# Moving the next pair's transposes and differences inside a Strassen-form pair of products (two graph layers, one Trainium2 core)

## Chip, cores and metric

The kernel runs on one core of one Trainium2 chip. The metric is the device time of one execution in microseconds. Six runs of the kernel before gave a median of 1068.01 us (1065.46 to 1069.62).

## The reference, cut to what matters

There are 2708 nodes with 1024 features in f32 and a sparse 0/1 adjacency matrix.

```
q, k, v = x@W_q.T + b_q, x@W_k.T + b_k, x@W_v.T + b_v
z    = where((q@k.T / 32) * adj == 0, -10000, (q@k.T / 32) * adj)
x    = layernorm(x + relu(softmax(z, axis=1) @ v))          # layer 0
x    = layernorm(x + adj @ (x @ weight) + bias)             # layer 1
```

## The kernel before, in words

**Staging.** The rows of `adj` become lists of column numbers, and the rows are sorted by how many they have, into 22 blocks of 128 rows (`SLOTS` is the list length that each block allows: 15 for block 0, down to 0 for block 21). Attention is computed only on listed neighbours: their rows of x are fetched by indirect gathers on GpSimd (POOL, `gather_slot`, L349), scored on VectorE (DVE, L813) and summed with their weights (L870). Layer 1 gathers rows of the layer-0 result `x1_d` and sums them (`sum_rows`, L1226, DVE L1238 and L1241). The weighted row sum r of a block is then multiplied by a 1024 x 1024 weight matrix on TensorE (PE).

**From one row sum to a product.** `flip` (L709) turns r: eight PE transposes of 128 x 128 into two PSUM tiles `tr` (L716), each copied by ScalarE (ACT) to the tile rT (L717). `tr` has three buffers in all (`p_tr`), rT two for each place in a pair.

**Pairs.** Most blocks are multiplied two at a time. `turn_pair` (L977) turns both row sums and then forms four matrices on DVE, `s_all` (L988 to L991, S[0] to S[3]) from the quarters a11, a12 (first block's rT) and a21, a22 (second block's). `s_all` has one buffer. `pair_products` (L1013) makes seven half products of four f32 matmuls each, into four PSUM banks, in the order a11·w11, a12·w21, S[1]·t2, S[0]·t1, S[2]·t3, S[3]·w22, a22·t4; w are quarters of the weights and t differences of them. Behind several of them DVE reads a bank: `add` (L1009, L1011) or `whole` (L1011 in layer 0, L1278 in layer 1). S[1]·t2 accumulates in the bank of a11·w11, so it may start only when `add(to[0][0], pa, base[0][0])` (L1022) has read that bank. In layer 1 the `base` is xr, the block's own row of x1 added on top of the bias: ACT copies the bias to xr (L1251), and POOL adds the gathered row (L1252).

**Order.** In layer 0 the list `steps` (L1089) ends with seven pairs, here pair 0 to pair 6: (7,20), (19,18), (17,8), (16,11), (15,10), (9,14), (13,12). In each step the loop (L1119) finishes the pair before (`finish_pair`), runs gather jobs, turns the blocks of this step and of the next (L1149), and only then emits this pair's products. In layer 1 the list `units` (L1221) has unit 0 (block 20 alone) and ten pairs, unit 1 to unit 10. Step i (L1309) finishes unit i-1, turns unit i+1, fetches xr of unit i+1, emits the row sums of unit i+3, and then the products of unit i.

The program is written with a framework that orders each engine's instructions itself: every instruction has a priority by its place in the program, an earlier one first, and `tc.high_priority(URGENT)` lifts some, such as `add`. An instruction is put into its engine's queue when its inputs and its buffers are free by the framework's own estimate of time; on the chip each queue then runs in that order. So the place in the program is a preference, and the trace shows what came of it. SyncE (SP) only starts the weight and bias loads here.

Of the kernel before, what the change touches and what calls it, by code (L numbers as in the profile page):

```python
# [80 lines left out]
def sparse_part(ctx, tc, x, xT, adj, wqT, wkT, wvT, bq, bk, bv, w1, b1, out):  # L81
# [29 lines left out]
    with es:  # L111
# [863 lines left out]
        halves_turned = []  # L975

        def turn_pair(flips, pool):  # L977

            A = []
            for k, flip_to in enumerate(flips):  # L980
                rT = (pool if k else wp).tile([P, DC, P], F32, name="rT", bufs=2)
                A.append(flip_to(rT))
            if len(flips) == 1:
                return A, None
            (a11, a12), (a21, a22) = [(a[:, :DC // 2], a[:, DC // 2:]) for a in A]
            s_all = wm_pool.tile([P, 4, DC // 2, P], F32, name="s_all", tag="m3")
            S = [s_all[:, i] for i in range(4)]
            nc.vector.tensor_add(S[0], a21, a22)  # L988
            nc.vector.tensor_sub(S[1], S[0], a11)
            nc.vector.tensor_sub(S[2], a11, a21)  # L990
            halves_turned.append(nc.vector.tensor_sub(S[3], a12, S[1]))  # L991
            return A, S

        def differences():
            return [wm_pool.tile([P, DC // 2, HALF], F32, name=f"t{k}", tag=f"m{k - 2}") for k in (2, 3, 4)]
# [14 lines left out]
            with tc.high_priority(URGENT):  # L1010
                nc.vector.tensor_add(to, acc, what)  # L1011

        def pair_products(A, S, w, ts, base, to, whole, first_alone=False):  # L1013

            (w11, t1), (w21, w22) = w
            t2, t3, t4 = ts
            (a11, a12), a22 = halves_of_turned(A[0]), halves_of_turned(A[1])[1]
            pa, pb, pc = bank(), bank(), bank()  # L1020
            half_products(pa, a11, w11, stop=False)
            add(to[0][0], pa, base[0][0])  # L1022
            half_products(pb, a12, w21)
            whole(0, 0, pb, to[0][0])
            if first_alone:
                half_products(pc, S[0], t1, stop=False)
                add(to[1][1], pc, base[1][1])
                half_products(pa, S[1], t2, start=False, stop=False)
                add(to[0][1], pa, base[0][1])
                half_products(pc, S[3], w22, start=False)  # L1030
                whole(0, 1, pc, to[0][1])
                half_products(pa, S[2], t3, start=False)
                whole(1, 1, pa, to[1][1])
                pd = bank()
                add(to[1][0], pa, base[1][0])
                products.append(half_products(pd, a22, t4))
                whole(1, 0, pd, to[1][0])
# [12 lines left out]
        def halves_of_turned(a):  # L1050
            return a[:, :DC // 2], a[:, DC // 2:]

        def project_pair(pair, A, S):
            ts = [(xb_pools[0] if k else wp).tile([P, D], F32, name="t", bufs=2 + k) for k in range(2)]
            bias = halves_of(bias_bc)

            def whole(k, h, acc, what):
                add(halves_of(ts[k])[h], acc, what)

            pair_products(A, S, wv_q, wv_t, [bias, bias], [halves_of(t) for t in ts], whole, pair == pairs[-1])  # L1060
            return ts

        def finish_pair(pair, ts):
# [44 lines left out]
        def turn0(b):  # L1108
# [3 lines left out]
                return rT  # L1112
            return flip_shares([got["hub"], got[0]]) if b == 0 else flip(got[b])

        credit = -STEP
        turned, done0 = {}, set(last)
        pending = None
        left_y = NB - FAMILY
        for i, (kind, b) in enumerate(steps):  # L1119
            if pending is not None:  # L1120
                pending[0](*pending[1:])
                credit -= END * (2 if pending[0] is finish_pair else 1)
                pending = None
            credit += STEP if kind != "p" else 2 * STEP - P_END
            step[0] = i
            for entry in joining[:]:
                if i >= entry[1] + 2:
# [12 lines left out]
            for c in [c for st in steps[i:i + 3] for c in blocks_of(st) if not (left_y and c in late)]:  # L1140
                while c not in done0 and c not in got and c != 0:
                    credit -= run_job()
            while 0 in jobs and i >= 15:
                credit -= run_job()
            while jobs and credit > 0 and len([c for c in got if c not in done0 and c not in ALONE and c != "hub"]) < (RB - 1 if left_y else RB):
                if left_y and len(jobs) <= late_jobs:
                    break
                credit -= run_job()
            for k, c in steps[i:i + 2]:  # L1149
                if k != "y" and c not in turned and not (left_y and k == "p"):  # L1150
                    turned[c] = turn0(c) if k == "v" else turn_pair([lambda rT, r=got[b_]: flip(r, rT) for b_ in c], xb_pools[0])
                    done0.update(blocks_of((k, c)))
            if kind == "y":
                if b == NB - 5:
                    row_constants(1)
                y_block(b)
                credit -= Y_END
                left_y -= 1
                if left_y == 0:
                    xa.release()  # L1160
                    xb_pool = tc.alloc_tile_pool(name="xb", bufs=1, side="right", reuse_waits="tile")
                    xb_pools.append(xb_pool)
                    xb_bc.append(xb_pool.tile([P, D], F32, name="xb_bc"))
                    bcast_rows(xb_bc[0], xbT)
            elif kind == "v":
                xr = gather_x(x, b)
                pending = finish0, b, (project_mean if b in last else project)(turned[b], wv_q), xr
            else:
                for b_ in b:
                    pair_x[b_] = gather_x(x, b_)  # L1170
                pending = finish_pair, b, project_pair(b, *turned[b])
        w1_q = quarters_of("w1")
        for i in range(2):
            for j in range(2):
# [96 lines left out]
        def work1(unit, A, S, xrs):  # L1271
# [14 lines left out]
            if S is None:  # L1286
                (a11, a12), x0 = halves_of_turned(A[0]), xs_[0]
                pa, pb = bank(), bank()
                half_products(pa, a11, w11, stop=False)
                add(x0[1], pa, x0[1])  # L1290
                half_products(pb, a11, t1, stop=False)
                half_products(pb, a12, w22, start=False)
                whole(0, 1, pb, x0[1])
                half_products(pa, a12, w21, start=False)
                whole(0, 0, pa, x0[0])
            else:
                pair_products(A, S, w1_q, w1_t, xs_, xs_, whole, unit == units[-1])
# [5 lines left out]
        turned1[0] = turn1(units[0], got1.pop(0))  # L1303
        follow(nc.vector.tensor_sub(t1, t1, w11), firsts[0], same=True)
        nc.vector.tensor_sub(t2, w22, t1)
        nc.vector.tensor_sub(t3, t2, w11)
# [2 lines left out]
        for i, unit in enumerate(units):  # L1309
            for p in pending:  # L1310
                finish1(*p)
            if i + 1 < len(units):
                turned1[i + 1] = turn1(units[i + 1], got1.pop(i + 1))
                xrs[i + 1] = [gather_x1(b, k) for k, b in enumerate(units[i + 1])]
            if i == 0:
                got1[2] = [sum_rows(b, k, halves_turned[-1]) for k, b in enumerate(units[2])]
            if i + 3 < len(units):
                got1[i + 3] = [sum_rows(b, k) for k, b in enumerate(units[i + 3])]
            if i == 4:
                sum_rows("hub")  # L1320
            pending = list(zip(unit, *work1(unit, *turned1.pop(i), xrs.pop(i))))
            if i == 2:
                for b in last:
                    pending.append((b, gather_x1(b), None))
# [319 lines left out]
```

## Time and profile before

The profiled execution took 1067.15 us, of which the span that the profile shows is 1065.4 us; 1.75 us lie around it.

| stretch of the span | what it is | PE busy | DVE busy | POOL busy |
|---|---|---|---|---|
| 558.00 to 746.00 (188.00 us) | layer 0, seven pairs | 184.36 us | 162.50 us | 95.86 us |
| 746.00 to 757.85 (11.85 us) | between the layers | 0.17 us | 4.46 us | 4.57 us |
| 757.85 to 860.00 (102.15 us) | layer 1, units 0 to 3 | 96.67 us | 80.68 us | 79.27 us |
| 860.00 to 960.60 (100.60 us) | layer 1, units 4 to 7 | 96.97 us | 80.71 us | 81.40 us |
| 960.60 to 1047.90 (87.30 us) | layer 1, rest of unit 7 to unit 10 | 87.25 us | 43.43 us | 32.91 us |

Busy time is the time in which an engine worked on an instruction. The timeline lists instructions in order with the time at which they began, how long they (or a run of equal ones) took, and in brackets how long the engine stood idle before and which instruction released it. An f32 matmul appears as two records, so a half product of four matmuls is a row with x8, and a turned block is a row with x8 of L716. POOL shows an idle time of 0.30 us or 0.31 us between two indirect gathers even when nothing holds it.

### The profile page before, as it was taken

The numbers are of one execution on the slowest core, as the hardware profiler recorded it, in microseconds if no ns is written. First come the engines' busy times: TensorE is split into PE (matmuls) and PEld (weight loads), VectorE is DVE, ScalarE is ACT, GpSimd is POOL, SyncE is SP. The second block draws the span as 40 slices with busy tenths as digits, with TensorE's granted clock in tenths as the row PEclk, the third lists the DMA queues.
The fourth block names the chain that finished last, engine by engine and source line by source line (L and its number), as shares of the span: only waits on it lengthen the run. The fifth ranks groups of instructions, "written<-read, shape, count | busy, mean of one in ns | idle before, by whom it ended". The sixth has DMA issues, their size and how long they took to land.

```text
span 1065.4 us, 10216 instructions
## 1 busy us (share of the span) xinstructions
PE 1005.1 (94%) x2849; PEld 473.7 (44%) x2849; DVE 849.6 (80%) x1831; ACT 425.6 (40%) x894; POOL 496.6 (47%) x397
## 2 busy tenths in 40 slices
PE   7999999999999999999999999999589999999993
PEld 6444444444443444444544444444334444454441
DVE  8799999994288889999399999965677877896532
ACT  4688788422042332214424343332323353333321
POOL 1000140057655445526157666511677787887300
PEclk9999999999999999999999999999799999999997
DMA  9555458565887656796433777726689589979701
GB/s 361 191 205 202 167 208 287 160 220 164 293 258 245 223 184 206 219 355 191 152 126 100 244 240 264 252 80 224 167 280 264 183 285 305 291 214 309 204 40 42
DMA packets 90962, 229.20 MB, mean 215 GB/s; under 512 B 18410, under 2 KB 40394, under 8 KB 88188
## 3 DMA queue, kind: packets, MB, share of 16 engines
q0 software_dynamic: 48768, 148.05, 43.6%
q1 hardware_dynamic: 42128, 80.41, 21.7%
q8 instruction: 24, 0.39, 0.1%
q14 instruction: 42, 0.34, 0.1%
HBM read 219.61 MB, written 33.68 MB: 238 GB/s over the span
## 4 chain that ended last, share of the span: by engine, by line
PE 18%; DVE 15%; issue 8%; DMA 5%; POOL 3%; ACT 1%; POOLq 0%; DVEq 0%
PE po L999 16%; DMA g<-x_d,tabs 3%; DVE r L870 3%; DVE junkv L813 2%; DVE r L1241 2%; DVE t L1011 1%; DMA yg<-y_d,tabs 1%; POOL g L349 1%; PE tr L716 1%; POOL xr L343 1%; DVE part L1241 1%; DMA g<-in_x_dram,tabs 1%; PE po L739 1%; PE tr L729 1%; POOL r L349 1%
## 5 line engine op out<-in xcount | busy, mean ns | idle before, releaser
L319 PE MATMUL po<-m_sb,xt 128*128 128x512 f32 x672 | 292.1, 593 | 3.2 <-DVE yo L323 3.2
L319 PEld LDWEIGHTS po<-m_sb,xt 128*128 128x128 f32 x672 | 126.5, 190 | 159.3 <-issue 151.1
L813 DVE SCALAR_TENSOR_TENSOR junkv<-yg,g 128x1024 uint8<-128x1024 f32 x109 | 132.9, 1219 | 32.4 <-DMA g<-in_x_dram,tabs 14.8
L349 POOL DMA_INDIRECT g<-in_x_dram,tabs x86 | 111.8, 1300 | 70.2 <-ACT r L868 20.0
L999 PE MATMUL po<-t,s_all 128*128 128x512 f32 x272 | 123.2, 595 | 4.0 <-DVE xr L1011 4.0
L1241 DVE SCALAR_TENSOR_TENSOR r<-g,valid,r 128x1024 f32<-128x1024 f32 x77 | 98.5, 1280 | 24.9 <-DMA g<-x_d,tabs 24.4
L609 PE MATMUL po<-wk_o,wq_o 128*128 128x512 f32 x256 | 110.5, 592 | 0.0
L739 PE MATMUL po<-wv,rT 128*128 128x512 f32 x224 | 97.7, 593 | 3.1 <-DVE pr L855 2.5
L775 ACT ACTIVATE junks<-t,lnm 128x1024 uint8<-128x1024 f32 (+1 forms) x41 | 47.0, 1146 | 127.2 <-DVE lnm L773 97.6
L349 POOL DMA_INDIRECT g<-x_d,tabs x67 | 78.6, 1174 | 22.7 <-issue 14.0
L563 POOL DMA_INDIRECT tab_d<-rec,pos_i x22 | 27.1, 1231 | 129.8 <-DVE pos_i L552 123.4
L870 DVE SCALAR_TENSOR_TENSOR r<-g,pr,r 128x1024 f32<-128x1024 f32 x64 | 81.8, 1279 | 5.8 <-ACT r L882 4.6
L999 PE MATMUL po<-w,rT 128*128 128x512 f32 x192 | 86.4, 599 | 0.0
L332 ACT ACTIVATE junka<-xt 128x128 f32<-128x128 f32 x176 | 53.8, 306 | 75.3 <-PE po L319 56.8
L788 ACT ACTIVATE t<-t,nmr,rstd 128x1024 f32<-128x1024 f32 (+1 forms) x41 | 50.0, 1237 | 81.2 <-DVE nmr L787 81.1
L999 PEld LDWEIGHTS po<-t,s_all 128*128 128x128 f32 x272 | 50.9, 190 | 70.5 <-issue 58.1
L224 DVE MAX8 few<-a 128x8 f32<-128x75 f32 (+3 forms) x132 | 79.2, 617 | 0.0
L609 PEld LDWEIGHTS po<-wk_o,wq_o 128*128 128x128 f32 x256 | 48.3, 190 | 59.3 <-issue 59.1
L999 PE MATMUL po<-w,s_all 128*128 128x512 f32 x160 | 72.1, 592 | 0.0
L221 DVE SCALAR_TENSOR_TENSOR a<-a,iota 128x2708 f32<-128x2708 f32 (+1 forms) x22 | 65.2, 2963 | 5.4 <-ACT junk L220 5.4
L739 PEld LDWEIGHTS po<-wv,rT 128*128 128x128 f32 x224 | 42.2, 190 | 56.0 <-issue 54.9
L717 ACT COPY rT<-tr 128x512 f32<-128x512 f32 x80 | 43.1, 586 | 52.8 <-PE tr L716 52.6
(350 smaller groups left out, 1524.4 us busy)
## 6 DMA issues: line engine op xcount, KB each, us to landing
a<-in_adj_dram SPq DMA_DIRECT2D x21, 1354.0 KB, 5.8
xt<-in_xT_dram SPq DMA_DIRECT2D x21, 512.0 KB, 5.2
y_d<-yo SPq DMA_DIRECT2D x21, 512.0 KB, 5.8
g<-in_x_dram SPq DMA_DIRECT2D x21, 512.0 KB, 7.9
wq_i<-in_wqT_dram SPq DMA_DIRECT2D x8, 512.0 KB, 8.8
wk_i<-in_wkT_dram SPq DMA_DIRECT2D x8, 512.0 KB, 10.4
wv<-in_wvT_dram SPq DMA_DIRECT2D x16, 256.0 KB, 5.6
w<-in_w_dram SPq DMA_DIRECT2D x4, 1024.0 KB, 7.6
```

What stands on the lines that cost most here:

```text
L221: nc.vector.scalar_tensor_tensor(a[:n], a[:n], 1.0, iota[:n], op0=ALU.is_equal, op1=ALU.mult)
L224: nc.vector.max(few[:n, i * 8:(i + 1) * 8], a[:n, cuts[i]:cuts[i + 1]])
L319: put = nc.tensor.matmul(po, xt[:, c, :], m_sb[c // 2][:, c % 2, k0:k1], start=(c == 0), stop=(c == DC - 1))
L332: put = nc.scalar.activation(junka, xts[b][:, c, :], AF.Copy, accum_out=xs[:, c, b:b + 1])
L349: nc.gpsimd.indirect_dma_start(out=dst[:n], out_offset=None, in_=src, in_offset=bass.IndirectOffsetOnAxis(ap=at, axis=0), bounds_check=N - ...
L609: nc.tensor.matmul(po, wq_o[i // 2][:, o, i % 2 * P:(i % 2 + 1) * P], wk_o[:, o, hs], start=(o == 0), stop=(o == DC - 1))
L739: put = nc.tensor.matmul(acc, rT[:, c, :], w[c // 4][h][:, c % 4, :], start=(c == 0), stop=(c == DC - 1))
L788: applied.append(nc.scalar.activation(t[:n], t[:n], AF.Identity, bias=nmr[:n], scale=rstd[:n]))
L813: nc.vector.scalar_tensor_tensor(junkv[:n], yg[:n, :D], scale, xg[:n], op0=ALU.mult, op1=ALU.mult, accum_out=s)
L870: nc.vector.scalar_tensor_tensor(r[:n], xg[j][:n], pr[:n, j:j + 1], r[:n], op0=ALU.mult, op1=ALU.add)
L999: put = nc.tensor.matmul(acc, a[:, k], w[:, k], start=start and k == 0, stop=stop and k == DC // 2 - 1, skip_group_check=True)
L1241: put = nc.vector.scalar_tensor_tensor(r[:n], xg[:n], ok[:n, j:j + 1], r[:n], op0=ALU.mult, op1=ALU.add)
```

## The change

The transposes of the next pair move from ahead of this pair's products to a place inside them, behind a12·w21 (`between()`). The four differences of the next pair move behind all of this pair's products (`pair_sums`). In layer 1 this puts the differences of unit i+1 behind the row sums of unit i+3 in the program; in step 0 the row sums of units 2 and 3 now both come behind the products of unit 0 and are tied to follow the last difference of unit 1 on DVE. The single unit 0 gets `between()` behind its first half product. No instruction is added or dropped.

```diff
-        def pair_products(A, S, w, ts, base, to, whole, first_alone=False):
+        def pair_products(A, S, w, ts, base, to, whole, between, first_alone=False):
...
             half_products(pb, a12, w21)
             whole(0, 0, pb, to[0][0])
+            between()
...
             for k, c in steps[i:i + 2]:
-                if k != "y" and c not in turned and not (left_y and k == "p"):
-                    turned[c] = turn0(c) if k == "v" else turn_pair([lambda rT, r=got[b_]: flip(r, rT) for b_ in c], xb_pools[0])
-                    done0.update(blocks_of((k, c)))
+                if k == "v" and c not in turned:
+                    turned[c] = turn0(c)
+                    done0.add(c)
+            if kind == "v" and steps[i + 1][0] == "p":
+                turned[pairs[0]] = turned_pair(pairs[0])
+                sums0[pairs[0]] = pair_sums(turned[pairs[0]])
...
-                pending = finish_pair, b, project_pair(b, *turned[b])
+                following = steps[i + 1][1] if i + 1 < len(steps) else None
+                pending = finish_pair, b, project_pair(b, turned[b], sums0[b], lambda: turned.update(
+                    {following: turned_pair(following)} if following else {}))
+                if following:
+                    sums0[following] = pair_sums(turned[following])
...
                 add(x0[1], pa, x0[1])
+                between()
                 half_products(pb, a11, t1, stop=False)
...
             if i + 1 < len(units):
-                turned1[i + 1] = turn1(units[i + 1], got1.pop(i + 1))
                 xrs[i + 1] = [gather_x1(b, k) for k, b in enumerate(units[i + 1])]
-            if i == 0:
-                got1[2] = [sum_rows(b, k, halves_turned[-1]) for k, b in enumerate(units[2])]
-            if i + 3 < len(units):
+            if 0 < i < len(units) - 3:
                 got1[i + 3] = [sum_rows(b, k) for k, b in enumerate(units[i + 3])]
             if i == 4:
                 sum_rows("hub")
-            pending = list(zip(unit, *work1(unit, *turned1.pop(i), xrs.pop(i))))
+            pending = list(zip(unit, *work1(unit, turned1.pop(i), sums1.pop(i), xrs.pop(i), lambda: turned1.update(
+                {i + 1: turn1(units[i + 1], got1.pop(i + 1))} if i + 1 < len(units) else {}))))
+            if i + 1 < len(units):
+                sums1[i + 1] = pair_sums(turned1[i + 1])
+            if i == 0:
+                for u in (2, 3):
+                    got1[u] = [sum_rows(b, k, halves_turned[-1]) for k, b in enumerate(units[u])]
```

`pair_sums` holds the old second half of `turn_pair`, L985 to L992, unchanged; `turned_pair` marks the pair's blocks as done and calls `turn_pair`.

More of the change, by code (lines that the diff above doesn't have):

```diff
@@ L982, in turn_pair, with pair_sums @@
                 A.append(flip_to(rT))
-            if len(flips) == 1:
-                return A, None
+            return A
+        def pair_sums(A):
+            if len(A) == 1:
+                return None
             (a11, a12), (a21, a22) = [(a[:, :DC // 2], a[:, DC // 2:]) for a in A]
@@ L991, in turn_pair @@
             halves_turned.append(nc.vector.tensor_sub(S[3], a12, S[1]))
-            return A, S
+            return S
         def differences():
@@ L1051, in halves_of_turned, with project_pair @@
             return a[:, :DC // 2], a[:, DC // 2:]
-        def project_pair(pair, A, S):
+        def project_pair(pair, A, S, between):
             ts = [(xb_pools[0] if k else wp).tile([P, D], F32, name="t", bufs=2 + k) for k in range(2)]
@@ L1058, in whole @@
                 add(halves_of(ts[k])[h], acc, what)
-            pair_products(A, S, wv_q, wv_t, [bias, bias], [halves_of(t) for t in ts], whole, pair == pairs[-1])
+            pair_products(A, S, wv_q, wv_t, [bias, bias], [halves_of(t) for t in ts], whole, between, pair == pairs[-1])
             return ts
@@ L1113, in turn0, with turned_pair @@
             return flip_shares([got["hub"], got[0]]) if b == 0 else flip(got[b])
+        def turned_pair(pair):
+            done0.update(pair)
+            return turn_pair([lambda rT, r=got[b_]: flip(r, rT) for b_ in pair], xb_pools[0])
+        sums0 = {}
         credit = -STEP
@@ L1269, in turn1, with work1 @@
                               for b, r in zip(unit, rs)], cp)
-        def work1(unit, A, S, xrs):
+        def work1(unit, A, S, xrs, between):
             ts = [wp.tile([P, D], F32, name="t", tag="t" if k % 2 == 0 else "yg") for k, _ in enumerate(unit)]
@@ L1296, in work1 @@
             else:
-                pair_products(A, S, w1_q, w1_t, xs_, xs_, whole, unit == units[-1])
+                pair_products(A, S, w1_q, w1_t, xs_, xs_, whole, between, unit == units[-1])
             return ts, sums
@@ L1303, in sparse_part @@
         turned1[0] = turn1(units[0], got1.pop(0))
+        sums1 = {0: pair_sums(turned1[0])}
         follow(nc.vector.tensor_sub(t1, t1, w11), firsts[0], same=True)
```

## The prediction

> **What bounds the kernel now.** I read the engine totals first, then the 40 slices, then PE's waits in the two pair stretches, then the timelines of PE, DVE, ACT and POOL there.
>
> ```profile
> PE 1005.1 (94%) x2849; PEld 473.7 (44%) x2849; DVE 849.6 (80%) x1831; ACT 425.6 (40%) x894; POOL 496.6 (47%) x397
> ...
> PE   7999999999999999999999999999589999999993
> ...
> POOL 1000140057655445526157666511677787887300
> ```
>
> PE is busy nearly everywhere, and since the change adds and drops no instruction, it can only win PE's idle gaps or open new ones. PE's waits from 558 to 1048 us (total, times, longest) say what gaps there are:
>
> ```profile
> PE tr L716 <- DVE r L1238: 12.2, 2, 11.7
> PE po L999 <- DVE xr L1011: 4.0, 4, 2.0
> PE tr L716 <- DVE r L870: 2.9, 4, 1.3
> PE tr L716 <- ACT rT L717: 2.0, 1, 2.0
> PE tr L716 <- DVE r L1241: 2.0, 1, 2.0
> PE tr L729 <- DVE r L1241: 0.6, 1, 0.6
> ```
>
> The 11.7 is the seam between the layers, where the last scatter and first gathers run; the change doesn't touch it. What remains, 12.2 + 4.0 + 2.9 + 2.0 + 2.0 + 0.6 - 11.7 = 12.0 us, is about the most that can be won (stretched records hide a little more, as in unit 0 below).
>
> PE's timeline of layer 0 (pairs 4 and 5) shows where:
>
> ```profile
> 666.34 3.60 PE L999 MATMUL po<-wv,rT 128*128 128x512 f32 x8
> 671.16 1.06 PE L716 MATMUL tr<-ident,r 128*128 128x128 f32 x8 [1.23 <-DVE r L870]
> 672.06 1.88 PE L999 MATMUL po<-wv,rT 128*128 128x512 f32 x4
> 674.15 1.07 PE L716 MATMUL tr<-ident,r 128*128 128x128 f32 x8 [0.21 <-DVE r L870]
> ...
> 695.49 3.60 PE L999 MATMUL po<-wv,rT 128*128 128x512 f32 x8
> 700.36 1.06 PE L716 MATMUL tr<-ident,r 128*128 128x128 f32 x8 [1.27 <-DVE r L870]
> 701.25 3.60 PE L999 MATMUL po<-wv,rT 128*128 128x512 f32 x8
> 704.69 3.60 PE L999 MATMUL po<-t,s_all 128*128 128x512 f32 x8
> ```
>
> A half product takes 704.69 - 701.25 = 3.44 us, a turned block 701.25 - 700.36 = 0.89 us. In pair 5 PE stands before the transposes of block 12, whose sum isn't ready, while a12·w21 of pair 5, which needs nothing more, is queued behind them. From 704.69 to the end of layer 0 PE runs without a gap, so a microsecond won here is won at the seam.
>
> In layer 1 POOL matters as well:
>
> ```profile
> 825.20 1.01 POOL L703 DMA_INDIRECT out_dram<-t,tabs  x1 [2.70 <-ACT t L788]
> ...
> 852.38 1.93 POOL L703 DMA_INDIRECT out_dram<-t,tabs  x1 [1.96 <-ACT t L788]
> ...
> 952.82 1.63 POOL L343 DMA_INDIRECT xr<-x_d,tabs  x1 [0.31 <-issue]
> ```
> ```profile
> 959.26 0.69 DVE L1011 TENSOR_TENSOR xr<-po,xr 128x512 f32<-128x512 f32 x1 [2.81 <-DMA xr<-x_d,tabs]
> ```
> ```profile
> 960.63 3.60 PE L999 MATMUL po<-t,s_all 128*128 128x512 f32 x8
> ```
>
> From 754.77 us on POOL issues with its minimal 0.30 us between gathers, except for four longer waits before out_dram scatters: 0.75, 2.70, 1.96 and 0.40 us, so 0.45 + 2.40 + 1.66 + 0.10 = 4.6 us above the minimum. Its xr gather of unit 7 at 952.82 lands for the DVE add at 959.26, and only then may S[1]·t2 of unit 7 run, at 960.63. From there PE has no gap until the end. So what PE wins earlier in layer 1 is waited off at unit 7 unless POOL gets there earlier too. Row sums do not help past it: block 0's are done at about 955.5.
>
> **The change, part by part.** *Layer 0, transposes behind a12·w21: -3.4 us.* Take pair 4 from its own start, 666.34: two half products to 673.22, block 9 (its sum came at 671.16) to 674.11, block 14 waits for its sum as before, 674.15, and ends at 675.05 with S[1]·t2 next. That was at 676.77, so 1.72 us sooner; the end of the pair at 694.12 becomes 692.4. Pair 5: two half products to 699.28, block 13 to 700.17, block 12 not before its sum, 700.36, to 701.25. S[1]·t2 starts there instead of at 704.69: 3.44 us sooner, one whole half product put under the wait. What is late next is the same sum of block 12: its chain runs over yg at 679.42, scores, and two L870 of 1.28 us, not over PE, so I leave it where it is. The rT slots cost nothing: turning pair i+1 overwrites pair i-1, which is finished in both orders. The tiles r are freed some 7 us later; three buffers rotate, and the tightest reuse (block 13's first write at 690.18, into block 10's place) lies 40 us behind that block's transposes.
>
> *Layer 1, transposes behind a12·w21: PE gains that units 6 and 7 eat.* S[1]·t2 must wait for the add on a11·w11's bank. Before, that add has a half product (3.44 us) to hide under; now 3.44 + 2 x 0.89 = 5.2 us. That covers PE's waits on xr of 1.99, 0.54 and 0.93 us (790.36, 843.78, 899.39); the fourth, 0.50 at 797.99, is for S[2]·t3 and stays. The 1.99 us before transposes of unit 2 (780.44) also go, and some 2.3 us in unit 0, whose four products from 759.6 now run up to block 18's sum. PE could thus reach unit 6 about 7.7 us sooner (1.99 + 0.54 + 0.93 + 1.99 + 2.3). But xr of unit 6, issued at 915.63, is used at 923.05, and unit 7's at 952.82 as above: by POOL's queue alone the end gains 0. If PE's earlier finish takes away all of POOL's 4.6 us of waiting, it gains 4.6. These waits are for ACT's normalisations, which follow DVE steps that stand between row sums, not PE alone. I take half, 2.3 us, and keep both ends.
>
> *Differences moved behind the products: 0.* Four DVE operations of 0.68 us, next to one another every 0.60 us, 2.4 us in all. `s_all` has one buffer, so before too they ran only after S[3]·w22 of the pair ahead. They have until S[1]·t2: a22·t4, two half products and now two turned blocks, 3 x 3.44 + 1.78 = 12.1 us. In layer 1 they now stand behind the sums of unit i+3. The stretch holds three adds of about 0.7 us, so 12.1 - 2.4 - 2.1 = 7.6 us is room for six sums of 1.2 us each. The trace shows four or five sums in the worst such stretch (unit 7's differences, 942.59 to 950.4, mixed with block 0's sums, which already had the better place). Bounds: 0, and 2.4 us a unit if eight sums got in front. I take 0.
>
> *POOL and the differences.* In the trace the gathers beside S operations at 805.55 and 832.40 take 0.99 us, the usual value, so moved differences cost POOL nothing. The Trainium skill (SBUF — State Buffer, Practical consequences) says a DVE instruction with two SBUF inputs blocks a GpSimd instruction that reads SBUF; by that rule each of the four could hold a gather for 0.68 us, up to 2.7 us a pair. The row shows no such hold, and it decides.
>
> *Transposes in one run: +0.5 us.* Two blocks now pass one after the other through three `tr` buffers, so the fourth tile waits for ACT's first copy (0.59 us). Without competition the row at 808.40 shows 1.93 us for 16, no stall. Beside other ACT work the trace has 0.26 us (889.41 took 2.19) and 2.02 us (867.12, ACT wait). The new place, 6.9 to 8.6 us after a pair's start, meets ACT's normalisations (L788 at 982.24, two for 2.37 us, stands 6.8 us into unit 8). Bounds 0 and 2.0 a pair, where it counts: pairs 0 to 5, and units 7 to 9, behind POOL's hold. I take 0.5 in all, twice the 0.26 row.
>
> *Queues and start of layer 1.* POOL's order by program place is unchanged but for units 2 and 3, whose gathers now come behind unit 0's products; their sums' tie to unit 1's last difference (773 us) precedes the first such sum (774.63). SP: no issue moves. No wait is added.
>
> Sum: -3.4 - 2.3 + 0.5 = -5.2. The profiled execution took 1067.15 us (span 1065.4 + 1.75), which gives 1061.9; the median of the runs, 1068.01, gives 1062.8. I forecast **1062.3**.
>
> **The rivals.** *POOL holds layer 1 entirely*: only -3.4 is left, 1063.7 from the profiled time, 1064.6 from the median. For: POOL's unbroken 0.30 us gaps from 853 to 992. Against: its waits at 825 and 852 hang on a PE that comes sooner.
> *POOL's waits all go and no copy collides*: -3.4 - 4.6 = -8.0; and 0.9 for the two records of unit 8's first product that PE may put before unit 7's hold: 1067.15 - 8.9 = 1058.2.
> *It doesn't do what it says*: the order is the framework's. The trace has block 9's transposes in the middle of pair 4's first two products, not ahead of them. If it places them by readiness again, or if block 12's sum slips by 3 us, nothing changes: 1067.
> *Slower, copies*: `tr` tiles behind ACT's normalisations in nine places (pairs 0 to 5, units 7 to 9). At 1.2 us each (half of 2.37), +10.8 - 3.4 - 2.3 = +5.1: 1072.3. It turns to slower when the mean stall passes 5.7 / 9 = 0.63 us. Against: ACT is busy 71.91 of 188 us in layer 0, so most tiles find it free.
>
> **How the numbers follow.** Forecast 0.38, POOL holds 0.22, all gained 0.12, no change 0.13, slower 0.15. Measurement can tell about 0.2%, 2.1 us, from no change. Faster: 0.38 + 0.22 + 0.12 = 0.72; same 0.13; slower 0.15. The range runs from just below the all-gained case, 1057, through no change to the start of slower, 1070, and leaves out most of the slower case and a little below.
>
> **What would show it.** Right: in pairs 4 and 5 the transposes stand behind 16 records of wv,rT and S[1]·t2 of pair 5 starts near 701.3; the seam is 3.4 us sooner; no wait on xr of a microsecond before S[1]·t2 in unit 1; POOL's waits before scatters in units 1 and 2 smaller; PE idle before S[1]·t2 of units 6 or 7 waiting for xr. Wrong: PE waits on ACT rT inside the transposes, S operations ending after PE wants them, block 12's sum later than 700.4, or xr gathers in another place in POOL's queue.

## The result, and the profile after

The changed kernel took 1075.31 us (median of 35 runs, 1071.45 to 1081.95), the kernel before 1068.42 us beside it (median of 72, 1063.53 to 1077.57). The ratio is 1.007, 95% interval 1.006 to 1.0081: **0.7% slower**, where 1062.3 us and "faster" were forecast. The profiled execution of the changed kernel took 1076.47 us (span 1074.7), that of the kernel before 1067.15 us (span 1065.4).

In what follows L1002 is the products' line (L999 before), L1014 their add (L1011), L1258 the row sum of layer 1 (L1241), L1268 the copy of the bias into xr on ACT (L1251); L716, L717, L775 to L788 are where they were. The turned blocks are `tr` (written by PE at L716), copied to `rT` by ACT at L717.

The engine totals of the page show no added work:

```profile
PE 1008.3 (94%) x2849; PEld 476.4 (44%) x2849; DVE 851.3 (79%) x1831; ACT 424.7 (40%) x894; POOL 501.1 (47%) x397
```

PE's waits from the first pair to the end of layer 1 (total, times, longest) do show a difference; two rows of 0.5 and 0.3 us are left out:

```profile
PE tr L716 <- ACT rT L717: 14.0, 8, 5.2
PE tr L716 <- DVE r L1255: 11.7, 1, 11.7
PE po L1002 <- DVE xr L1014: 3.5, 2, 2.9
```

The change did what it meant to: the waits for row sums (r L870 2.9, r L1241 2.0 and 0.6) are gone, and only the seam's 11.7 us is left of them. In their place stand eight waits for a copy, 14.0 us where there had been one of 2.0. PE's timeline of pairs 4 and 5 answers to the one in the prediction:

```profile
668.55 7.03 PE L1002 MATMUL po<-wv,rT 128*128 128x512 f32 x16
675.42 2.20 PE L716 MATMUL tr<-ident,r 128*128 128x128 f32 x16
677.46 3.60 PE L1002 MATMUL po<-t,s_all 128*128 128x512 f32 x8
...
695.42 7.03 PE L1002 MATMUL po<-wv,rT 128*128 128x512 f32 x16
702.29 1.47 PE L716 MATMUL tr<-ident,r 128*128 128x128 f32 x12
703.60 1.02 PE L1002 MATMUL po<-t,s_all 128*128 128x512 f32 x2
705.94 0.66 PE L716 MATMUL tr<-ident,r 128*128 128x128 f32 x4 [1.32 <-ACT rT L717]
```

Both half products now run ahead of the turns, as written. But the turns break after three tiles (x12), and the fourth (x4) waits 1.32 us until ACT has emptied the first. (That the trace puts two product records ahead of the fourth tile is the framework's order.) Where the turns break, they break in this way; the waits are 0.19, 1.43 and 1.32 us in pairs 0, 3 and 5, and 1.90, 5.17, 0.99, 0.51 and 2.53 us in units 1 to 5 of layer 1. At all eight places a step of a norm stands directly ahead of the copies on ACT.

**Why the copy is late.** Unit 2, the worst place: PE, then ACT, then DVE of the changed kernel.

```profile
809.42 7.03 PE L1002 MATMUL po<-w,rT 128*128 128x512 f32 x16
816.28 1.47 PE L716 MATMUL tr<-ident,r 128*128 128x128 f32 x12
822.92 1.11 PE L716 MATMUL tr<-ident,r 128*128 128x128 f32 x4 [5.17 <-ACT rT L717]
823.83 5.78 PE L1002 MATMUL po<-t,s_all 128*128 128x512 f32 x8
```
```profile
820.59 1.15 ACT L775 ACTIVATE junks<-t,lnm 128x1024 uint8<-128x1024 f32 x1 [3.88 <-DVE lnm L773]
821.65 0.19 ACT L775 ACTIVATION_READ_ACCUMULATOR junks<-t,lnm 128x1 f32 x1
821.87 0.29 ACT L778 ACTIVATE lv<-vs,eps 128x1 f32<-128x1 f32 x1
822.19 0.20 ACT L780 ACTIVATE near<-lv 128x1 f32<-128x1 f32 x1
822.30 1.54 ACT L717 COPY rT<-tr 128x512 f32<-128x512 f32 x3
```
```profile
811.95 1.29 DVE L1258 SCALAR_TENSOR_TENSOR r<-g,valid,r 128x1024 f32<-128x1024 f32 x1 [5.06 <-DMA g<-x_d,tabs]
813.15 0.68 DVE L991 TENSOR_TENSOR s_all<-rT 128x512 f32<-128x512 f32 x1
...
817.96 0.68 DVE L994 TENSOR_TENSOR s_all<-rT,s_all 128x512 f32<-128x512 f32 x1
...
819.16 1.27 DVE L1258 SCALAR_TENSOR_TENSOR r<-g,valid,r 128x1024 f32<-128x1024 f32 x1
820.36 0.20 DVE L773 TENSOR_SCALAR lnm<-sm,sm 128x1 f32<-128x1 f32 x1
```

Read from below. DVE stood 5.06 us for a gather. The mean of the unit before (lnm), 0.20 us of work, stands in DVE's queue behind that row sum, three more, and the four moved differences (L991 to L994, 0.68 us each), and came at 820.36. In the kernel before, three of the four ran ahead of this gather, at 805.78 to 807.68. ACT stood idle 3.88 us for it, because the norm (L775) is at the head of its queue; the copies, whose tiles had been ready since 817.75 (816.28 + 1.47), stand behind it. So three queues that work in order, one behind the other, carry a late gather to PE, and ACT is idle, not busy, while PE waits for it. The Trainium skill (Perfetto Trace Analysis, section Tensor Engine Instruction (MATMUL, LD_WEIGHTS)) says that ACT and DVE take their instructions strictly in order; these rows agree: no copy starts before L780 has (822.19, then 822.30). In the kernel before, ACT had the same copies in front of the norms:

```profile
809.03 2.05 ACT L717 COPY rT<-tr 128x512 f32<-128x512 f32 x4 [2.09 <-PE tr L716]
810.95 1.08 ACT L1251 COPY xr<-bias 128x1024 f32<-128x1024 f32 x1
814.04 1.15 ACT L775 ACTIVATE junks<-t,lnm 128x1024 uint8<-128x1024 f32 x1 [2.01 <-DVE lnm L773]
```

There the turns stand ahead of the two half products, some 7 us earlier in the unit, and their copies ahead of the norms. ACT's order is the framework's; it followed the turns' new place.

**What a wait costs besides itself.** The product behind the 5.17 us took 5.78 us instead of 3.60. The windows of that stretch (length, then busy time of PE, PEld, DVE, ACT, POOL, then the granted TensorE clock, DMA share, GB/s):

```profile
823.80:829.50 5.70, 5.70 (x11) 2.40 (x10) 3.92 (x6) 2.27 (x6) 2.82 (x2) 0.61 0.99 214
829.50:835.00 5.50, 5.50 (x14) 2.42 (x13) 3.08 (x8) 2.37 (x2) 2.43 (x3) 1.00 0.41 168
```

After the wait the clock was granted at 0.61 for one half product, which cost another 2.2 us; then it was whole again.

The sum: layer 1, from the end of the seam's wait to its last matmul, took 298.5 us against 290.2: +8.3. PE's waits there, without the seam's, went from 9.1 (0.5 + 4.0 + 2.0 + 2.0 + 0.6) to 14.6 us (11.1 of the 14.0, + 3.5): +5.4 before rounding. The clock adds 2.6 at unit 2 (turns 0.91 us instead of 0.49, product 5.62 instead of 3.44, by their starts) and 1.7 after unit 5's 2.53 us (four records in 3.05 us instead of 1.72, the next product in 3.80 instead of 3.44). Against these 4.3 us the kernel before has more small delays: over all of PE's records in the stretch, what they took beyond the median of their kind went from 6.3 to 9.2 us, +2.9. 5.4 + 2.9 is the 8.3 measured. The pairs of layer 0, from the first S product to the seam, took 175.1 us against 175.6.

### The profile page after: what moved, and what is told of

It is laid out like the page before. It is cut to its first block, busy times and chain, and to the rows that moved or that the text cites. A ratio compares the mean times of both kernels' runs of the same rounds, so it can differ in the third digit from the quotient of the medians.

```text
span 1074.7 us, 10224 instructions
## 1 busy us (share of the span) xinstructions
PE 1008.3 (94%) x2849; PEld 476.4 (44%) x2849; DVE 851.3 (79%) x1831; ACT 424.7 (40%) x894; POOL 501.1 (47%) x397
## 4 chain that ended last, share of the span: by engine, by line
PE 21%; DVE 11%; issue 7%; DMA 6%; POOL 4%; ACT 1%; POOLq 0%; DVEq 0%
PE po L1002 18%; DVE r L870 3%; DMA g<-x_d,tabs 2%; POOL g L349 2%; DVE junkv L813 2%; DMA yg<-y_d,tabs 2%; DVE t L1014 1%; PE po L739 1%; POOL xr L343 1%; DMA out_dram<-t,tabs 1%; DVE r L1258 1%; PE tr L716 1%; DVE t L1074 1%; PE tr L729 1%; DMA xr<-x_d,tabs 1%
## 5 line engine op out<-in xcount | busy, mean ns | idle before, releaser
L1002 PE MATMUL po<-t,s_all 128*128 128x512 f32 x272 | 127.0, 608 | 3.5 <-DVE xr L1014 3.5
L1258 DVE SCALAR_TENSOR_TENSOR r<-g,valid,r 128x1024 f32<-128x1024 f32 x77 | 98.6, 1281 | 18.6 <-DMA g<-x_d,tabs 18.0
L775 ACT ACTIVATE junks<-t,lnm 128x1024 uint8<-128x1024 f32 (+1 forms) x41 | 47.0, 1146 | 128.7 <-DVE lnm L773 96.7
L349 POOL DMA_INDIRECT g<-x_d,tabs x67 | 83.7, 1249 | 22.8 <-issue 15.9
L870 DVE SCALAR_TENSOR_TENSOR r<-g,pr,r 128x1024 f32<-128x1024 f32 x64 | 81.8, 1279 | 5.5 <-ACT r L882 4.6
L1002 PE MATMUL po<-w,rT 128*128 128x512 f32 x192 | 86.1, 601 | 0.0
L788 ACT ACTIVATE t<-t,nmr,rstd 128x1024 f32<-128x1024 f32 (+1 forms) x41 | 50.4, 1239 | 77.9 <-DVE nmr L787 77.8
L1002 PEld LDWEIGHTS po<-t,s_all 128*128 128x128 f32 x272 | 51.1, 195 | 61.5 <-issue 55.7
L1002 PE MATMUL po<-w,s_all 128*128 128x512 f32 x160 | 72.8, 595 | 0.0
L716 PE MATMUL tr<-ident,r 128*128 128x128 f32 x320 | 42.8, 280 | 26.1 <-ACT rT L717 14.0
```

The source lines that it names most:

```text
L349: nc.gpsimd.indirect_dma_start(out=dst[:n], out_offset=None, in_=src, in_offset=bass.IndirectOffsetOnAxis(ap=at, axis=0), bounds_check=N - ...
L716: nc.tensor.transpose(tr[:, k, :], r[:, c * P:(c + 1) * P], ident)
L870: nc.vector.scalar_tensor_tensor(r[:n], xg[j][:n], pr[:n, j:j + 1], r[:n], op0=ALU.mult, op1=ALU.add)
L1002: put = nc.tensor.matmul(acc, a[:, k], w[:, k], start=start and k == 0, stop=stop and k == DC // 2 - 1, skip_group_check=True)
L1258: put = nc.vector.scalar_tensor_tensor(r[:n], xg[:n], ok[:n, j:j + 1], r[:n], op0=ALU.mult, op1=ALU.add)
```

## The experiments

Theory A: the loss comes from the place of the copies. Two blocks turned in one run need four `tr` tiles, there are three, and the fourth waits for a copy that now stands behind the norms on ACT. Its rivals were B (POOL's queue is late in layer 1, and the waits on rT only fill time in which PE would wait for something else), C (the moved differences S are late), and, from what the first four runs showed, D (the gathers pace layer 1 through DVE's queue, so a wait that is taken away comes back at the next add) and E (S and the norms' means stand behind one or two more row sums on DVE).

All results at once; each ratio is to the kernel before on the same chip. "Pairs" runs from the first S product to the seam, "layer 1" from the seam's end to the last matmul, both of one profiled execution; "on rT" is PE's wait for copies from the turns of the second pair on, in us. The stretches of "before" are those of its one profile, of 1067.15 us; e1 to e4, e5 to e8 and e9 to e12 ran on three chips where that kernel took 1079.5 to 1081.4 us and was not profiled.

| kernel | ratio, 95% interval | pairs | layer 1 | on rT |
|---|---|---|---|---|
| before | 1 | 175.6 | 290.2 | 2.0 |
| changed | 1.007, 1.006 to 1.0081 | 175.1 | 298.5 | 14.0 |
| changed, once more (e12) | 1.0059, 1.0029 to 1.0090 | 175.4 | 299.3 | 7.8 |
| layer 0 only (e3) | 0.9990, 0.9961 to 1.0019 | 175.5 | 296.9 | 3.3 |
| layer 1 only (e4) | 1.0055, 1.0029 to 1.0081 | 175.6 | 297.0 | 7.0 |
| differences only (e5) | 1.0028, 1.0012 to 1.0044 | 175.4 | 293.4 | 4.0 |
| turns parted (e6) | 0.9994, 0.9979 to 1.0009 | 173.5 | 291.4 | 0.4 |
| changed, 4 tr (e1) | 0.9961, 0.9932 to 0.9989 | 173.2 | 295.5 | 0 |
| before, 4 tr (e2, e11) | 0.9918, 0.9884 to 0.9951; 0.9944, 0.9917 to 0.9972 | 173.3; 173.7 | 288.5; 288.5 | 0 |
| differences only, 4 tr (e10) | 0.9941, 0.9916 to 0.9966 | 173.6 | 291.4 | 0 |
| turns parted, 4 tr (e9) | 0.9925, 0.9898 to 0.9952 | 172.5 | 291.5 | 0 |
| changed, half the gathers (e7) | 1.0057, 1.0036 to 1.0078 | 174.3 | 302.9 | 13.9 |
| before, half the gathers (e8) | 1.0034, 1.0020 to 1.0048 | 175.7 | 300.6 | 0.8 |

Layer 1 of a single execution varies: e3 has the layer 1 of the kernel before and shows 296.9 us in its profile, with two waits on xr of 8.9 us in all, though its median is level with before. So a difference of 3 to 7 us between two of these stretches proves nothing by itself; the ratios decide, and the stretches only say where to look.

**A fourth tr buffer (e1, e2).** The kernel's eight buffers in PSUM were 4 `po`, 3 `tr` and 1 `mm`; the one `mm` is given up.

```
-p_tr = es.enter_context(tc.tile_pool(name="p_tr", bufs=3, space=PSUM))
-p_mm = es.enter_context(tc.tile_pool(name="p_mm", bufs=1, space=PSUM))
+p_tr = es.enter_context(tc.tile_pool(name="p_tr", bufs=4, space=PSUM))
...
-mm = p_mm.tile([P, HALF], F32, name="mm")
+mm = p_tr.tile([P, 4, P], F32, name="tr").rearrange("p a b -> p (a b)")
```

> The changed kernel with four tr buffers in PSUM in place of three (the one mm buffer is given up, its few users take a tr tile), so that both blocks of a pair can be turned without any copy of ACT having been made. Theory A (the fourth tr tile waits for ACT's first copy, which stands on ACT behind the norms of the pair before): PE's waits on ACT rT, 14.0 us in the changed kernel, fall below 2 us, the clock drops inside units 2 and 5 go with them, and the time is 1058 to 1064. Theory B (layer 1 is late because POOL's queue is late, the waits on rT only fill time in which PE would have waited for xr or row sums anyway): the waits on rT go as well, but waits on xr or r of nearly the same length come in their place and the time stays at 1071 to 1076. Theory C (the moved differences S are late): waits on DVE s_all stay or grow, 1071 to 1076.

> The kernel before with the same fourth tr buffer: a control for what the buffer is worth by itself. Its PE waits on ACT rT are one of 2.0 us, and it never turns more than three tiles against a late copy. Theories A, B and C all give 1066 to 1069, the time before within 2 us. If it is faster by over 3 us, the buffer helps for a reason of its own and the first run doesn't show theory A.

On this chip the kernel before took 1080.91 us, so A's 1058 to 1064 stands for 0.990 to 0.996 of it. The changed kernel came to 0.9961, at the edge of that; by the ratios 1.1% (12 us) of what it takes with three buffers was gone, and with it every wait on rT in the two stretches. PE's waits there:

```profile
PE po L1002 <- DVE xr L1014: 11.9, 8, 5.5
PE tr L716 <- DVE r L1255: 11.7, 1, 11.7
PE tr L716 <- DVE r L870: 0.8, 1, 0.8
```

That is A's gain in time, but also B's picture in layer 1: 11.9 us on the adds for xr came in the place of the copies. And the control was not level, as all theories had said: the kernel before gained 0.8% from the buffer. So these two runs show that the copies' waits can be bought off, not that they were the whole difference, which with four buffers is still 0.4% (0.9961 against 0.9918) or 0.2% (against 0.9944, below). The intervals overlap there. In the profiles little of the gain is where A puts it: layer 1 of e1 took 295.5 us, 3.0 less than with three buffers and 7.0 more than that of e2.

**One layer at a time (e3, e4).** e3 turns, sums and forms differences in layer 1 as before; e4 does so in layer 0. The edit of e4, shortened (e3 likewise puts the lines of the loop over `units` back):

```
 if following:
+    turned[following] = turned_pair(following)
+    sums0[following] = pair_sums(turned[following])
-pending = finish_pair, b, project_pair(b, turned[b], sums0[b], lambda: turned.update(...))
-if following:
-    sums0[following] = pair_sums(turned[following])
+pending = finish_pair, b, project_pair(b, turned[b], sums0[b], lambda: None)
```

> The change in layer 0 alone: layer 1 turns, sums and forms differences where the kernel before did. Theory A: waits on rT of 0.2, 1.4 and 1.3 us against a gain of 3.4 at the start of S[1]t2 of pair 5, so 1067.5 to 1068.5 against 1068.4, about no change. Theory B says the same of layer 0, and C too unless S is late there; all of the 7 us must then show in the run with layer 1 alone.

> The change in layer 1 alone: layer 0 is that of the kernel before. Theory A: five waits on rT of 0.5 to 5.2 us (11 us) and two clock drops of 2 us, less the waits on row sums and xr that go (about 6 us): 1074 to 1077. Theory B: the same time, 1074 to 1077, but then POOL's xr gather for unit 7 is 8 to 9 us later than before and PE stands before S[1]t2 of units 6 or 7 on xr. If it is below 1071, layer 0 carries part of the loss and both theories are wrong on the place.

Layer 0 alone is level (0.9990), layer 1 alone carries the loss (1.0055, 5.9 us at 1080.9). The place is settled. In e4 the waits on rT were 7.0 us, where A had said 11, and those on xr 5.3, so B was still alive; but its own sign did not come: POOL's xr gather of unit 7 was 2.1 us later than before (197.1 us after the seam instead of 195.0), not 8 to 9, and the waits on xr were in units 1 and 5, not 6 or 7.

**Only the differences (e5).** The call that turns the next pair goes back ahead of the products:

```
 pa, pb, pc = bank(), bank(), bank()
+between()
 half_products(pa, a11, w11, stop=False)
 ...
 whole(0, 0, pb, to[0][0])
-between()
...
```

In layer 1 this call still comes behind xr's fetch and the row sums of unit i+3 in the program, where the kernel before turns first, so e5 is not quite the kernel before with the differences moved.

> The changed kernel with the turned blocks put back ahead of the pair's first product; only the differences S stay behind the pair's products. DVE's queue then has the differences of unit 2 behind 14 to 16 row sums of layer 1 instead of 13 to 14, and the adds of the products where the kernel before has them. Theory A (copies behind norms, because two blocks are turned in one run at the new place): waits on ACT rT as in the kernel before (one of about 2 us), time within 0.2% of before. Theory E (S and the norms' sums on DVE stand behind one or two more row sums, each of which waits for a gather): waits on DVE s_all or rT at units 2 and 3 of 2 to 4 us together, 0.2 to 0.4% slower than before.

0.28% slower, E's number. But its one wait on rT of 4.0 us was at unit 4, where the kernel before has its one of 2.0, not at units 2 and 3, and no wait on S appeared. e10 below takes this up again.

**The turns parted (e6).** The sharpest test of A, since it changes neither buffers nor the place of the first turn:

```
-whole(0, 0, pb, to[0][0])
-between()
+whole(0, 0, pb, to[0][0])
+between(0)
 ...
 half_products(pa, S[1], t2, start=False, stop=False)
 add(to[0][1], pa, base[0][1])
+between(1)
 half_products(pc, S[0], t1, stop=False)
```

> The changed kernel with the two blocks parted: the first is turned behind a12 w21 as changed, the second one half product (3.44 us) later, so that at most two tr tiles are written in a row. Theory A: waits on ACT rT fall from 14.0 to below 3 us, the time lies within 0.3% of the kernel before, as with four tr buffers, or below it. Theory D (layer 1 is paced by the gathers: DVE adds stand in its queue behind row sums that wait for gathers, and a wait that is taken away at the copies comes back at the next add): the waits on rT go, waits on DVE xr grow to 8 to 12 us, and layer 1 from the seam to its last matmul still takes 295 to 298 us.

The whole loss is gone: 0.9994, with 0.4 us on rT. A's sign came in full, D's only at one place. The waits put down to xr are 2.6 us, but one more belongs to them, at unit 1: the trace calls it "issue", and it ends with xr's add on DVE (800.36 + 0.68 = 801.04). The product behind it ran at a lowered clock, 6.56 us instead of 3.60.

```profile
801.10 6.56 PE L1003 MATMUL po<-t,s_all 128*128 128x512 f32 x8 [3.46 <-issue]
```

That makes 6.1 us on xr where D had said 8 to 12, and layer 1 took 291.4 us, not 295 to 298. B falls with the time: nothing but the place of one turn was changed, POOL's waits ahead of scatters stayed nearly as long (5.8 us above the minimum of 0.30, 6.4 in the changed kernel), and the loss went all the same. C has found no wait on S in the changed kernel, in e4 or here. Unit 2, PE, then ACT, then DVE of this kernel:

```profile
822.10 7.03 PE L1003 MATMUL po<-w,rT 128*128 128x512 f32 x16
828.97 1.04 PE L716 MATMUL tr<-ident,r 128*128 128x128 f32 x8
829.84 3.60 PE L1003 MATMUL po<-t,s_all 128*128 128x512 f32 x8
833.28 1.04 PE L716 MATMUL tr<-ident,r 128*128 128x128 f32 x8
```
```profile
830.28 1.15 ACT L775 ACTIVATE junks<-t,lnm 128x1024 uint8<-128x1024 f32 x1 [3.88 <-DVE lnm L773]
...
831.99 1.05 ACT L717 COPY rT<-tr 128x512 f32<-128x512 f32 x2
```
```profile
821.63 1.28 DVE L1261 SCALAR_TENSOR_TENSOR r<-g,valid,r 128x1024 f32<-128x1024 f32 x1 [2.07 <-DMA g<-x_d,tabs]
```

ACT is idle the same 3.88 us behind the same mean, and the copies still come 2 us after the turn has ended (830.01, then 831.99), at no cost: two tiles fit into three buffers, and when the next two come, at 833.28, both copies are done (833.04). The place is not quite as hard as in the changed kernel, though. The gather held DVE for 2.07 us instead of 5.06, so the copies began 3.0 us after the turn's start instead of 6.0. Turned in one run, the fourth tile would by these rows have waited some 2.2 us here (an estimate: it starts 0.62 us after the first copy does, at 832.61, and three tiles end at 830.44); the rest of the 5.17 us went because the gather came sooner.

**Half the gathers (e7, e8).** Slots 1, 3, 5 ... of layer 1 are left out, with their row sums, in the changed kernel and in the one before; 58 of the 106 gathers for row sums are left, and POOL's queue there has 102 instructions instead of 150.

```
-for j in range(tab.shape[1] if b else J0):
+for j in range(0, tab.shape[1] if b else J0, 2):
```

> The changed kernel with every second gather and row sum of layer 1 left out (slots 1, 3, 5 ... of each block), so POOL has about half its queue there; the norms, copies, turns and products are the same. Theory A with the norms' own length as its cause: the norms still stand ahead of the copies on ACT, so waits on rT in layer 1 stay at 8 us or more (11.1 in the changed kernel). Theory D: the norms and adds are late only because DVE waits for gathers, so PE's waits on rT and xr in layer 1 fall from 14.6 to below 4 us in all and layer 1 takes 286 to 289 us from the seam.

> The kernel before with the same gathers and row sums of layer 1 left out: what the change costs or brings when the gathers don't pace layer 1. Theory D: layer 1 takes 286 to 289 us as in the changed kernel, and the two differ by under 2 us, the changed one ahead by what it wins in layer 0 or level. Theory A with the norms' own length: the changed kernel stays 5 to 8 us slower.

D's numbers did not come: with the shorter queue on POOL the waits on rT were 13.9 us in all, and layer 1 became longer, not shorter, in both kernels (302.9 and 300.6 us). But the gathers were not out of the way either: at unit 1 of e7 one gather still held DVE for 6.56 us, and PE then waited 6.63 us for a copy. What speaks against D is e6, not this pair. But A's own number failed too: the changed kernel was only 1.5 us slower (1084.8 against 1083.3), since the kernel before had lost 10.4 us on xr adds. Leaving work out gave both kernels another order of instructions, and the pair of runs says less than it was meant to. Why fewer gathers take longer stays open.

**With four buffers, what is left of the rest (e9, e10, e11), and the changed kernel again (e12).**

> The changed kernel with the two turned blocks parted by a half product and with four tr buffers. Theory A (the loss is the copies' place alone): no wait on ACT rT is left, and with parted turns the kernel before with four buffers (0.992 of before) is matched or beaten: 0.988 to 0.993. Theory E (the moved differences and the norms' sums keep a cost of their own, because they stand behind one or two more row sums on DVE): waits on DVE xr or t of 3 to 6 us stay in layer 1 and the ratio is 0.994 to 0.998.

> The kernel with only the differences moved, with four tr buffers. Theory E: the cost of the moved differences, 0.28% with three buffers, is the same with four: 0.992 plus 0.003, that is 0.994 to 0.997 of before. Theory A: moving the differences costs something only through copies that come late, so with four buffers it costs nothing: 0.991 to 0.993.

> The kernel before with four tr buffers once more, beside the two above. The first time it was 0.9918 of before (0.988 to 0.995). If the fourth buffer is worth that much by itself, it comes out at 0.989 to 0.995 again; if the first figure was the scatter of one chip, at 0.997 to 1.002.

> The changed kernel itself once more, on the chip of the three runs above, so that their ratios can be set against it: 1.005 to 1.008 of before, with waits on ACT rT of 10 to 15 us in all, the longest in units 1, 2 or 5 of layer 1. If it lies within 0.2% of before here, the loss depends on the chip and not on the copies.

e10 and e11 are level (0.9941, 0.9944): with four buffers no cost of moving the differences is seen. That is A's number and not E's, but each ratio is uncertain by 0.25% or more, so a cost of 0.28% isn't excluded, and layer 1 of e10's one profile is 2.9 us longer than e11's. That e5's 0.28% went through the copies is likely from its trace, not shown. e11 confirms that the fourth buffer is worth something to the kernel before: 0.6 to 0.8%, with intervals from 0.3 to 1.2%. e9 (0.9925) lies inside the same intervals: with four buffers the parted turns bring nothing that can be told from none. It has A's ratio but also E's sign, 7.8 us of waits on xr in layer 1, and the only wait on S of all runs, 0.7 us in the pairs. e12 repeats the loss (1.0059). Its 7.8 us on rT have 6.4 us more beside them, in waits of the same turns that its trace puts down to "issue" (5.0) and to lv, a step of the norm (1.4):

```profile
PE tr L716 <- ACT rT L717: 7.8, 4, 3.8
PE tr L716 <- issue: 5.0, 2, 4.9
PE po L1002 <- DVE xr L1014: 3.3, 2, 2.6
PE tr L716 <- ACT lv L778: 1.4, 1, 1.4
```
```profile
891.63 0.58 ACT L717 COPY rT<-tr 128x512 f32<-128x512 f32 x1 [5.66 <-remote]
```

The longest of these, 4.9 us at unit 4, is a fourth tile too, but its copy stood behind no norm: ACT had ended its last one 5.66 us before, and the trace does not name what the copy waited for ("remote").

Any of the kernels with four buffers beats both kernels of this case; the simplest is the kernel before with that one edit. Where its 0.6 to 0.8% (6 to 9 us) comes from was not followed up beyond this. Against the one profile of the kernel before, 1.9 to 2.3 us are in the pairs and 1.7 in layer 1; some lies ahead of the pairs, for on the same chip e1 and e2 reached the first S product at 579.1 and 580.4 us, e3 and e4 with three buffers at 583.5 and 581.4. What is left open is also whether the changed order with four buffers (0.9961) is really behind the old one (0.9918 and 0.9944). Not tested was the direct change of ACT's order: the copies lifted ahead of the norms, with turns and buffers as in the changed kernel.

## Why the prediction was wrong

- **Transposes in one run, +0.5 us: the step that failed.** It measured 14.0 us of waits, 1.75 at a mean of eight places, and 4.3 us of lost clock behind two of them. The mechanism was in the text (four tiles, three buffers, ACT's norms in between), and so was the rival "slower, copies", whose 1072.3 us is right in direction. But its places were not: of its nine, three had a wait, 2.9 us in all, which is 0.33 at a mean and below its own tipping point of 0.63, and units 7 to 9 had none. Three things in its sizing failed. The copies' delay was taken from how long norms *run* (2.37 us), not from how long they *wait*: in unit 2 ACT was idle for 3.88 us with the copies behind it, and the waits of 5.17 and 2.53 us lie above the bound of 2.0 a pair. The price was taken from the milder of two rows, 0.26 us, though the other, 2.02 us at 867.12, showed copies behind a norm's steps too; both are of turns at the old place, and the new place gave ACT's queue another order. And the count left out units 1 to 6 as hidden behind POOL, while five of the eight waits, 11.1 of the 14.0 us, were there.
- **"No wait is added"** was wrong for the same reason: the fourth tile's wait for a copy had been in the code all along, but PE met it once.
- **The clock** was not in the sum at all. The trace of before had the seam to show it: an 11.7 us wait, and the granted clock at 0.50 in the 3.3 us behind it and 0.75 in the next 3.4.
- **Layer 0, -3.4 us.** The order came as predicted (16 product records, then turns) and row-sum waits went, but the pairs took 175.1 us against 175.6, and e3 is level: the 2.9 us of waits for copies gave it back. With the turns parted they took 173.5: 2.1 us were there to be had.
- **Layer 1, PE's gain and POOL's -2.3 us.** The waits on row sums went, and two of those on xr, but what PE had won by S[1]·t2 of unit 1 (30.3 us after the seam instead of 32.5) was waited off in the same unit: the 0.50 us for S[2]·t3 that "stays" became 2.88, and PE stood 40.3 us after the seam where it had stood at 40.1. Then came unit 2's wait for the copy. The hold at unit 7 was there too, only later: xr's gather at 957.93 instead of 952.82, its add at 967.97 instead of 959.26, S[1]·t2 at 970.02, 211.3 us after the seam instead of 202.8. PE didn't stand there, for it had come 1.4 us later still; but without its waits for copies it would have stood for this xr. POOL's long waits ahead of scatters did not shrink: 0.95, 4.78 and 1.56 us are 6.4 us above the minimum of 0.30, where 4.6 had been and half was to go. PE before, then PE, POOL, DVE and again PE of the changed kernel:

```profile
797.99 3.70 PE L999 MATMUL po<-t,s_all 128*128 128x512 f32 x8 [0.50 <-DVE xr L1011]
```
```profile
799.01 3.70 PE L1002 MATMUL po<-t,s_all 128*128 128x512 f32 x8 [2.88 <-DVE xr L1014]
```
```profile
831.96 1.02 POOL L703 DMA_INDIRECT out_dram<-t,tabs  x1 [4.78 <-ACT t L788]
...
957.93 2.10 POOL L343 DMA_INDIRECT xr<-x_d,tabs  x1 [0.30 <-issue]
```
```profile
967.97 0.69 DVE L1014 TENSOR_TENSOR xr<-po,xr 128x512 f32<-128x512 f32 x1 [1.30 <-DMA xr<-x_d,tabs]
```
```profile
970.02 3.60 PE L1002 MATMUL po<-t,s_all 128*128 128x512 f32 x8
```

- **Differences, 0.** Right as far as the products go: the changed kernel shows no wait on S, and with four buffers e10 and e11 are level. But the sum priced only a late S, not what S makes late: in unit 2 the four stand ahead of the norm's mean, 2.4 us for which the copies then wait, and with three buffers the move nearly by itself (e5) measured 0.28%. That they cost POOL nothing was read from two rows and holds over more: in layer 1 of the changed kernel the 13 gathers with a difference in their first 0.5 us took 1.27 us in the mean, the other 93 took 1.24.
- **Two small misreadings.** PE's waits before have two more rows, 0.5 us for nms and 0.2 for junks, so 12.7 and not 12.0 us could be won at most; and POOL's gaps from 853 us on are not unbroken, for the wait of 0.40 us is at 859.2.
- **Direction and chances.** "Slower" had 0.15, with "ACT is busy 71.91 of 188 us" as the ground against. A busy share says how much work an engine has, not whether its queue's head is waiting. That argument carried the error; the changed kernel's ACT was busy for 424.7 us against 425.6 and held PE all the same.

## What to carry to other kernels

Before a producer's burst is moved, count its buffers against the burst: with n buffers the piece n+1 waits for the consumer's queue, and what counts there is not how busy the consumer is but what its queue's head waits for, followed back through every engine that works in order. Where the burst can't be drained in time, part it (half a product between the two turned blocks repaired all of this change) or give it one more buffer. Price a wait on TensorE from about 2 us on with the clock that may follow it (here 1.5 us or more behind most of those above 2.2), not with its length alone.

## What was not expected of the hardware

**The clock drops after short waits.** Over the profiles of all these kernels, in layer 1 after the seam: PE waits between 1.2 and 2.1 us left the product behind them at its usual length (3.6 to 3.7 us for eight records), but for one of 1.94 us (16 records in 8.73 us instead of 7.03). Of the 13 between 2.2 and 3.0 us five cost nothing (2.51, 2.56, 2.63, 2.79 and 2.88 us were followed by 3.70) and eight did: 2.21, 2.32, 2.43 and 2.97 us were each followed by 5.40, and behind 2.34, 2.39, 2.53 and 2.59 us, too, the records took 1.7 us more than usual. Every wait of 3.15 us or more, up to 6.63, was followed by a product of 4.7 to 6.7 us, so 1.5 to 3.1 us on top with the turns ahead of it. e1's 5.54 us is such a case, its clock 0.59 in the 6.2 us after it. The Trainium skill (TensorE: Matmul & The Clock Gate, section HAM oscillation — how this bites in real kernels) gives the rule as no idle gaps of PE above some 3.4 us; here the loss began at about 2 us, though not at each wait, so the measured bound is the lower one.
